# A two-layer convolution-style network on one core: the attention of two images written as one stage instead of two blocks

## The chip, the cores and the metric

One Trainium2 chip, one of its cores. The metric is device time in microseconds (us) of the whole kernel, one launch. Before the change the median of 3 runs is 4517.93 us (4510.86 to 4522.47).

## What is computed

The input x is [2, 256, 64, 64] in fp32: two images of 256 channels and L = 4096 positions. Layer 0 is a selective-scan block, layer 1 is attention with 8 heads of 32 channels, each behind a group norm and with a residual. Cut to what matters here:

```
def _gn(v, G=32, eps=1e-5):                 # per image: mean and variance of each group of 8 channels
    ...
    return ((g - m) / jnp.sqrt(s + eps)).reshape(v.shape)

x = x + _L0_conv_ref(_gn(x), ...)            # layer norm, projection, convolution, scan, gate, MLP
x = x + _L1_conv_ref(_gn(x), qkv_w, qkv_b, 8)

def _L1_conv_ref(x, qkv_w, qkv_b, num_heads):
    qkv = jnp.einsum('bchw,oc->bohw', x, qkv_w) + qkv_b[None, :, None, None]
    ...
    attn_logits = jnp.einsum('bhci,bhcj->bhij', q, k) * scale
    attn_weights = jax.nn.softmax(attn_logits, axis=-1)
    out = jnp.einsum('bhij,bhcj->bhci', attn_weights, v)
```

## The kernel before

**Layer 0** (`mamba_stage`, L257) works through 16 tiles of 512 positions, 8 of each image. All its work is registered as tasks with a cost, a due time and their data dependences (`Plan.add`, L134); `Plan.order` (L180) then simulates the engines and writes out one fixed order for each engine. An engine that stands in front of an instruction whose input is missing also holds everything behind it. Ahead of the plan, `first(0, t, 0)` (L328, L343) loads the 8 tiles of image 0 for the group statistics. The ring `yn` has three buffers (L304). Three small set-up inputs (`w_dt32`, `pick32`, `perm`, L369 to L375) borrow them, and the plan's own load of the first data tile (`front`, L493) takes the first that comes free. The 8 statistics tiles of image 1 (L875) and the late weights (`load_late`, L416) are SyncE tasks of the plan behind that load.

In the last tiles of image 1 the plan also has the group norm and the q, k and v projections of **image 0** for layer 1 (`qkv`, L686), which are written to DRAM scratch.

**Layer 1** is `attention_block` (L931), called twice. For image 0 it has `prepared=True` and loads what layer 0 wrote (`load_prepared`, L1059). For image 1 `prepare` (L985) first makes q, k and v from x: for each of 8 tiles, load x (`load_x`), normalise it with the group-norm scales (L998), project keys and queries (`project`, L1002: 8 matmuls each, q and k split into two halves and written to DRAM) and values (`project_values`, L1026). The tiles it uses are in a pool of its own, opened for the preparation.

Then comes a loop over S = 512 slots of one image. In a slot, TensorE makes the logits of four heads for one block of 128 keys and 512 queries (`logits`, L1098, two PSUM tiles of the ring `s`, which has three buffers) and multiplies the exponentials of the slot before with the values (`values`, L1137). ScalarE makes the exponentials (L1122), VectorE and GpSimd add up the softmax sums (`add_up`, L1151). 32 slots make an output tile. Its end (`finish`, L1178: sums, reciprocal, residual, store) is a generator which the loop advances by one piece in some of the later slots (`Slots`, L60).

The group-norm scales of image 1 (`group_norm_scales`, L30) are such a generator too, started in slot 34 of image 0 (L1217): two small matmuls and Ln and Exp on ScalarE (L56, L57).

All calls stand in `manual_schedule` blocks: within a block the order on each engine is the program's. Instructions of different blocks, and those outside any block, are interleaved by the framework. When a pool is closed, what is allocated there next waits until the old tiles' last users are done.

Of the kernel before, what the change touches and what calls it, by code (L numbers as in the profile page):

```python
# [19 lines left out]
P = 128  # L20
T = 512
# [8 lines left out]
def group_norm_scales(nc, small, psum_tile, stats, gmat, eps_t, out):  # L30

    KC = stats.shape[1]
    mv = [small.tile([P, 2], F32, name=f"gn_mv{k}") for k in range(KC)]
    e = [small.tile([P, 2], F32, name=f"gn_e{k}") for k in range(KC)]
    out += [small.tile([P, 2], F32, name=f"gn_sc{k}") for k in range(KC)]
    for k in range(KC):
        nc.vector.bn_aggr(mv[k], stats[:, k, :, :].rearrange("p a s -> p (a s)"))
    yield 3  # L40
    ps = psum_tile()
    for k in range(KC):
        nc.tensor.matmul(ps[:, 0, k : k + 1], lhsT=gmat, rhs=mv[k][:, 0:1], start=True, stop=True)
    for k in range(KC):
        nc.vector.tensor_copy(out[k][:, 0:1], ps[:, 0, k : k + 1])


    for k in range(KC):
        nc.vector.tensor_sub(e[k][:, 0:1], mv[k][:, 0:1], out[k][:, 0:1])
        nc.vector.scalar_tensor_tensor(e[k][:, 1:2], e[k][:, 0:1], e[k][:, 0:1], mv[k][:, 1:2], ALU.mult, ALU.add)  # L50
    yield 3
    ps = psum_tile()
    for k in range(KC):
        nc.tensor.matmul(ps[:, 0, k : k + 1], lhsT=gmat, rhs=e[k][:, 1:2], start=True, stop=True)
    for k in range(KC):
        nc.scalar.activation(e[k][:, 0:1], ps[:, 0, k : k + 1], AF.Ln, bias=eps_t)  # L56
        nc.scalar.activation(out[k][:, 1:2], e[k][:, 0:1], AF.Exp, scale=-0.5)  # L57
# [199 lines left out]
def mamba_stage(ctx, tc, xs, stats_out, consts, w, outs, scratch):  # L257
# [88 lines left out]


# [134 lines left out]
    def front(i):  # L482
# [4 lines left out]
        yn = d.yn = Buf(r_yn, KC)  # L487
# [5 lines left out]
        add("SP", due - 46, 1.7, lambda: nc.sync.dma_start(yn.tile, image_tile(xs[b], t)), [], [yn], lands=3.3)  # L493
# [437 lines left out]
def attention_block(ctx, tc, b, stats, consts, w, out, scratch, range_t, prepared, ahead):  # L931
# [9 lines left out]
    C, L = out.shape  # L941
# [4 lines left out]
    x = scratch.image(b)  # L946

    p2 = ctx.enter_context(tc.tile_pool(name=f"l1p2{b}", bufs=2))
    wp = ctx.enter_context(tc.tile_pool(name=f"l1w{b}", bufs=1))
    ps_s = ctx.enter_context(tc.tile_pool(name=f"l1pss{b}", bufs=3, space=PSUM))  # L950
    ps_2 = ctx.enter_context(tc.tile_pool(name=f"l1ps2{b}", bufs=1, space=PSUM))
    ps_o = ctx.enter_context(tc.tile_pool(name=f"l1pso{b}", bufs=1, space=PSUM))
# [8 lines left out]
    kp = ctx.enter_context(tc.tile_pool(name=f"l1k{b}", bufs=NT))  # L961
    ep = ctx.enter_context(tc.tile_pool(name=f"l1e{b}", bufs=5))
    ec = ctx.enter_context(tc.tile_pool(name=f"l1c{b}", bufs=2))
    keys = {}
    queries = {}

    def load_keys(g, t, queue=nc.sync):


        k = keys[g, t] = (kq if g and t == 0 else kp).tile([P, 4, T], F32R, name="k")  # L970
        load_stack(queue, k, scratch.qk[b * KG + g, 1, t], 1)

    def load_queries(i, queue=nc.sync):
        if i < KG * NT:
            g, t = divmod(i, NT)
            q = queries[i] = p2.tile([P, 4, T], F32R, name="q")
            load_stack(queue, q, scratch.qk[b * KG + g, 0, t], 0)
# [3 lines left out]


    FIRST = 3

    def prepare():  # L985

        w_qkv, gn = ahead
        with tc.tile_pool(name=f"l1p{b}", bufs=2) as pp:
            xn = {}

            def load_x(t):
                if t < NT:
                    xn[t] = pp.tile([P, KC, T], F32, name="xn")
                    nc.sync.dma_start(xn[t], x.rearrange("(k p) l -> p k l", p=P)[:, :, bass.ts(t, T)])

            def normalise(t):
                for c in range(KC):
                    nc.vector.tensor_scalar(  # L998
                        xn[t][:, c, :], xn[t][:, c, :], gn[c][:, 0:1], gn[c][:, 1:2], ALU.subtract, ALU.mult
                    )  # L1000

            def project(t, i):  # L1002


                pm = s_tile()
                for m in range(KC):
                    for c in range(KC):
                        nc.tensor.matmul(  # L1008
                            pm[:, m, :],
                            lhsT=w_qkv[:, c, bass.ds(i * C + m * P, P)],  # L1010
                            rhs=xn[t][:, c, :],
                            start=(c == 0),
                            stop=(c == KC - 1),
                        )
                halves = pp.tile([P, 2, KC, T], F32R, name="halves")
                for m in range(KC):
                    bias = b_qkv[:, i * KC + m : i * KC + m + 1]
                    nc.scalar.activation(halves[:, 0, m, :], pm[:, m, :], AF.Identity, bias=bias)
                    nc.vector.scalar_tensor_tensor(
                        halves[:, 1, m, :], pm[:, m, :], bias, halves[:, 0, m, :].bitcast(F32), ALU.add, ALU.subtract  # L1020
                    )
                    nc.sync.dma_start(
                        scratch.qk[b * KG + m, i, t].rearrange("s c h t -> (c h) s t"), halves[:, :, m, :].bitcast(F32)
                    )

            def project_values(t):  # L1026
                pm = s_tile()
                flat = pm.rearrange("p a t -> p (a t)")
                for j in range(T // P):
                    for c in range(KC):  # L1030
                        nc.tensor.matmul(
                            flat[:, bass.ts(j, C)],
                            lhsT=xn[t][:, c, bass.ts(j, P)],
                            rhs=w_qkv[:, c, 2 * C : 3 * C],
                            start=(c == 0),
                            stop=(c == KC - 1),
                        )
                nc.scalar.copy(v[:, bass.ts(t, T // P), :].rearrange("p s c -> p (s c)"), flat)

            with tc.manual_schedule():  # L1040
                load_x(0)
                load_x(1)
                normalise(0)
                for t in range(NT):
                    project(t, 1)
                    if t + 1 < NT:
                        normalise(t + 1)
                    project(t, 0)
                    project_values(t)
                    load_x(t + 2)  # L1050

                    if t == 1:
                        load_queries(0)
                    if 0 < t <= FIRST:
                        load_keys(0, t - 1)
                for t in range(FIRST, NT):
                    load_keys(0, t)

    def load_prepared():  # L1059
        def load_values(g, t, queue=nc.sync):  # L1060
            cs = bass.ts(t, T // P)
            queue.dma_start(v[:, cs, g * P : (g + 1) * P], scratch.v[b * KG + g, :, cs, :])

        with tc.manual_schedule():
# [11 lines left out]
    load_prepared() if prepared else prepare()  # L1076

    p1 = ctx.enter_context(tc.tile_pool(name=f"l1p1{b}", bufs=1))
    p3 = ctx.enter_context(tc.tile_pool(name=f"l1p3{b}", bufs=2))
    kq = ctx.enter_context(tc.tile_pool(name=f"l1kq{b}", bufs=1))  # L1080
# [8 lines left out]
    class Slot:  # L1089
        pass  # L1090

    S = KG * NT * NC
    SHARED = [c for c in range(8, NC) if c % 8 in (0, 2, 4, 5, 6)]
    todo = {}
    tiles = {}
    side = Slots()

    def logits(s, half):  # L1098
        if s >= S:
            return  # L1100
        i, c = divmod(s, NC)
        kt, kj = divmod(c * P, T)
        if half == 0:
            todo[s] = Slot()
            todo[s].s, todo[s].e = [], []
        ps = s_tile()
        for j in range(2):
            h = 2 * half + j
            nc.tensor.matmul(  # L1109
                ps[:, j, :], lhsT=keys[i // NT, kt][:, h, kj : kj + P], rhs=queries[i][:, h, :], start=True, stop=True  # L1110
            )
        todo[s].s.append(ps)

    def exponentials(s, half):
        if half == 0 and s % NC < NC - 1:
            k = place(s % NC)
            first = s % NC == 0 or k == 1 and s % NC > 1
            todo[s].chunk = (todo.pop("chunk", None) or chunk()) if first else todo[s - 1].chunk
            e = todo[s].chunk[:, k // 2, :, :, k % 2]
        else:  # L1120
            e = ep.tile([P, 2, T], F32, name="e")
# [303 lines left out]
```

## Time and profile before

| | |
|---|---|
| median of the runs | 4517.93 us |
| the profiled execution: its own time, its span | 4522.6 us, 4520.6 us |
| mean granted TensorE clock | 0.977 |
| busy share of the span: PE, DVE, ACT, POOL | 94%, 87%, 83%, 84% |
| layer 0, until the first logits | 0 to 2123.5 us |
| loop of image 0, until its last values matmul ends | 2123.5 to 3261.8 us |
| first to last matmul of the preparation of image 1 | 3280.7 to 3372.4 us |
| loop of image 1, first exponential to last values matmul | 3373.5 to 4502.2 us |
| end of the span | 4520.6 us |

PE is TensorE (PEld its weight loads), DVE is VectorE, ACT ScalarE, POOL GpSimd, SP SyncE, whose queue issues most transfers. In the time line each row is a start, a duration, an engine, a line of the kernel, an operation with its output and inputs, and in square brackets how long the engine had been idle and what ended that. In the chain each row is a start, a duration and what the end of the kernel was waiting for in that time. In the table by windows each engine has its busy time in the window; then come the granted clock, the busy share of the DMA engines and GB/s.

### The profile page before, as it was taken

To read this page: it belongs to the slowest core of one execution; us is meant where nothing else is said; L and a number is where in the kernel's file an instruction comes from. 1 tells how busy PE (TensorE), PEld (TensorE's weight loads), DVE (VectorE), ACT (ScalarE), POOL (GpSimd) and SP (SyncE) were. 2 spreads that over 40 slices of the span, in tenths; PEclk is the share of its full clock that TensorE was granted. 3 is DMA by queue.
4 is the path that set the end of the run, shared out by engine and by line. 5 is a ranking of instruction groups with operands and counts; after the bars stand their busy time and mean duration, and the time that the engine had idled before them with its cause. 6 is when DMAs were issued, how large, how long until landed. Compare 5 with 4: busy or idle time off the path is not lost.

```text
span 4520.6 us, 53932 instructions
## 1 busy us (share of the span) xinstructions
PE 4252.8 (94%) x18530; PEld 1637.9 (36%) x18530; DVE 3922.2 (87%) x3306; ACT 3766.1 (83%) x4842; POOL 3817.0 (84%) x2251
## 2 busy tenths in 40 slices
PE   5789999999999999988999999999899999999998
PEld 2233333333333333333333333333353333333333
DVE  4999999999999989894889889898838898898988
ACT  4788888888788888873999999999749999999997
POOL 2999999999999999994788888888718888888887
PEclk8899999999999999999999999999999999999999
DMA  5233333333443434446110040100081110401100
GB/s 192 94 115 104 111 124 121 127 126 127 143 155 132 139 122 143 140 151 168 32 27 23 22 102 17 26 24 22 10 262 50 45 28 18 101 17 26 29 20 8
DMA packets 173065, 389.24 MB, mean 86 GB/s; under 512 B 24176, under 2 KB 50544, under 8 KB 164592
## 3 DMA queue, kind: packets, MB, share of 16 engines
q1 hardware_dynamic: 171904, 383.37, 27.5%
q10 hardware_dynamic: 880, 2.36, 0.2%
q8 instruction: 147, 2.41, 0.2%
q14 instruction: 134, 1.10, 0.1%
HBM read 292.34 MB, written 93.32 MB: 85 GB/s over the span
## 4 chain that ended last, share of the span: by engine, by line
PE 64%; POOL 12%; DVE 9%; issue 6%; ACT 5%; DMA 3%; SPq 0%; POOLq 0%; DVEq 0%; ACTq 0%
PE s L1109 26%; PE po L1143 24%; PE mm L437 8%; POOL h L837 6%; DVE h L831 5%; POOL dbu L826 3%; PE y L863 2%; ACT L242 2%; ACT da L820 1%; DVE bn L826 1%; PE mm L669 1%; PE mm L633 1%; PE s L1008 1%; PE bn L437 1%; DMA dtu_rep<-dtu_dram 1%
## 5 line engine op out<-in xcount | busy, mean ns | idle before, releaser
L1135 DVE TENSOR_REDUCE chunk<-chunk 128x1024 f32<-128x4096 f32 x288 | 1269.8, 4409 | 217.0 <-ACT chunk L1122 217.0
L1176 POOL TENSOR_TENSOR acc_p<-acc_p,e 128x1024 f32<-128x1024 f32 x480 | 1150.9, 2398 | 148.5 <-ACT e L1122 129.2
L1122 ACT ACTIVATE chunk<-s 128x1024 f32<-128x1024 f32 x992 | 1117.1, 1126 | 181.6 <-PE s L1109 140.3
L837 POOL TENSOR_TENSOR h<-h,c 128x1024 f32<-128x1024 f32 x512 | 1206.0, 2365 | 40.3 <-ACT state L834 28.3
L1109 PE MATMUL s<-q,k 128*128 128x512 f32 x4096 | 1230.2, 422 | 6.7 <-ACT chunk L1122 3.1
L1143 PE MATMUL po<-chunk,v 128*32 128x512 f32 x3968 | 1112.9, 636 | 0.0
L1143 PE MATMUL po<-e,v 128*32 128x512 f32 x4224 | 1080.3, 605 | 0.0
L1122 ACT ACTIVATE e<-s 128x1024 f32<-128x1024 f32 x1056 | 1073.9, 1020 | 7.3 <-PE s L1109 6.6
L1109 PEld LDWEIGHTS s<-q,k 128*128 128x128 f32 x4096 | 689.5, 188 | 1009.9 <-issue 905.7
L820 ACT ACTIVATE da<-dt_rep,neg_a 128x512 f32<-128x512 f32 x1024 | 690.7, 701 | 131.9 <-DVE h L831 108.2
L1174 POOL TENSOR_TENSOR acc_p<-acc_p,e 128x512 f32<-128x512 f32 x480 | 629.4, 1311 | 162.7 <-ACT e L1122 140.0
L831 DVE TENSOR_TENSOR_SCAN h<-da,state,dbu 128x512 f32<-128x512 f32 x512 | 650.2, 1273 | 44.6 <-POOL dbu L826 41.5
L831 DVE TENSOR_TENSOR_SCAN h<-da,state,bn 128x512 f32<-128x512 f32 x512 | 646.7, 1263 | 11.6
L826 POOL TENSOR_TENSOR dbu<-dtu_rep,b 128x512 f32<-128x512 f32 x384 | 485.8, 1275 | 22.2 <-DMA dtu_rep<-dtu_dram 17.9
L242 ACT ACT_TABLE_LOAD x332 | 426.0, 1283 | 6.5 <-PEq L1415 0.7
L437 PE MATMUL bn<-proj,pick 112*128 112x512 f32 x512 | 294.4, 591 | 116.0 <-DVE h L831 115.4
L863 PE MATMUL y<-h,sum 128*32 128x512 f32 x2048 | 361.0, 633 | 40.0 <-POOL h L837 39.8
L826 DVE TENSOR_TENSOR bn<-dtu_rep,bn 128x512 f32<-128x512 f32 x512 | 348.2, 680 | 41.4 <-PE bn L437 24.0
L1173 DVE TENSOR_TENSOR acc<-acc,e 128x512 f32<-128x512 f32 x448 | 309.5, 691 | 24.2 <-ACT e L1122 13.9
L1143 PEld LDWEIGHTS po<-chunk,v 128*32 128x32 f32 x3968 | 142.9, 108 | 362.6 <-issue 351.3
L437 PE MATMUL mm<-yn,w_in 128*128 128x512 f32 x512 | 252.4, 619 | 10.3 <-ACT yn L526 9.1
L437 PE MATMUL mm<-yn,w 128*128 128x512 f32 x512 | 245.4, 609 | 8.0 <-ACT hid L658 5.7
(136 smaller groups left out, 4055.8 us busy)
## 6 DMA issues: line engine op xcount, KB each, us to landing
dt_rep<-dt_dram SPq DMA_DIRECT2D x128, 512.0 KB, 5.1
dtu_rep<-dtu_dram SPq DMA_DIRECT2D x128, 512.0 KB, 5.5
q<-qk_dram SPq DMA_DIRECT2D x124, 256.0 KB, 4.8
k<-qk_dram SPq DMA_DIRECT2D x62, 512.0 KB, 8.4
b<-bc_dram SPq DMA_DIRECT2D x64, 256.0 KB, 3.1
c<-bc_dram SPq DMA_DIRECT2D x64, 256.0 KB, 3.7
dt_dram<-dt SPq DMA_DIRECT2D x64, 256.0 KB, 2.0
dtu_dram<-lw SPq DMA_DIRECT2D x64, 256.0 KB, 2.5
```

Of the source, the lines that this page charges most:

```text
L242: self.nc.scalar.preload_act_table_set(self.TABLES[task.table])
L437: nc.tensor.matmul(out, lhsT=lhsT, rhs=rhs, start=(i == 0), stop=(i == len(pairs) - 1))
L820: nc.scalar.activation(da[j].tile, dt.tile[:, j, :], AF.Exp, scale=scale)
L826: engine.tensor_mul(out.tile, dtu.tile[:, j, :], rows.tile)
L831: nc.vector.tensor_tensor_scan(h.tile[:, j, :], da[j].tile, dbu.tile, initial, ALU.mult, ALU.add)
L837: nc.gpsimd.tensor_tensor(h.tile, h.tile, rows_c.tile.unsqueeze(1).to_broadcast([P, 2, T]), ALU.mult)
L1109: nc.tensor.matmul(ps[:, j, :], lhsT=keys[i // NT, kt][:, h, kj : kj + P], rhs=queries[i][:, h, :], start=True, stop=True)
L1122: nc.scalar.activation(e, todo[s].s[half], AF.Exp, scale=SCALE)
L1135: nc.vector.tensor_reduce(out, terms, AX.XY, ALU.add)
L1143: nc.tensor.matmul(tiles[i].po[h * D : (h + 1) * D, :], lhsT=v[:, c, g * P + h * D : g * P + (h + 1) * D], rhs=todo[s].e[h // 2][:, h % 2, :],
L1174: nc.gpsimd.tensor_add(acc_p[:, 1, :], acc_p[:, 1, :], eb[:, 1, :])
L1176: nc.gpsimd.tensor_add(acc_p, acc_p, eb)
```

## The change

The two calls become one function, `attention`, with one set of pools for both images and one `manual_schedule` block for the whole of layer 1. The preparation of image 1 no longer has a pool: its x tiles lie in a query buffer and in `e` buffers, its q and k halves in `chunk` buffers of the loop. Its first loads, first normalisation and first projection stand in the last slots of image 0's loop (`run`), and the first logits and exponentials of image 1 ahead of its last value projection. `finish` of image 0's last tile is advanced by the preparation (`side.run()`). The group-norm scales start in slot 1 of image 0 and use the PSUM buffer `a2`; a table set is preloaded on ScalarE at the head of the stage. At the end of `finish` the two range maxima come after the store, and the last product of the kernel is on VectorE. In layer 0 the load of the first data tile moves out of the plan, to just behind the 8 statistics loads of image 0.

```
@@ group_norm_scales
-    yield 3
+    yield 2
     ps = psum_tile()
...
-        nc.vector.scalar_tensor_tensor(e[k][:, 1:2], e[k][:, 0:1], e[k][:, 0:1], mv[k][:, 1:2], ALU.mult, ALU.add)
-    yield 3
+        nc.vector.tensor_mul(e[k][:, 1:2], e[k][:, 0:1], e[k][:, 0:1])
+        nc.vector.tensor_add(e[k][:, 1:2], e[k][:, 1:2], mv[k][:, 1:2])
+    yield 2
     ps = psum_tile()
...
+    yield
     for k in range(KC):
...
@@ mamba_stage
         for t in range(NT):
             first(0, t, 0)
 
+        first_yn = Buf(r_yn, KC)
+        first_yn.tile, first_yn.given = r_yn.make(), True
+        r_yn.given.append(first_yn)
+        nc.sync.dma_start(first_yn.tile, image_tile(xs[0], 0))
...
-        yn = d.yn = Buf(r_yn, KC)
+        yn = d.yn = Buf(r_yn, KC) if i else first_yn
...
-        add("SP", due - 46, 1.7, lambda: nc.sync.dma_start(yn.tile, image_tile(xs[b], t)), [], [yn], lands=3.3)
+        if i:
+            add("SP", due - 46, 1.7, lambda: nc.sync.dma_start(yn.tile, image_tile(xs[b], t)), [], [yn], lands=3.3)
@@ attention_block -> attention
+    def load_x(t):
+        if t >= NT:
+            return
+        if t < 2:
+
+            if t == 0:
+                xn["q"] = p2.tile([P, 4, T], F32R, name="q").bitcast(F32)
+            xn[t] = xn["q"][:, KC * t : KC * t + KC, :]
+        else:
+            xn[t] = ep.tile([P, KC, T], F32, name="e")
+        nc.sync.dma_start(xn[t], scratch.image(1).rearrange("(k p) l -> p k l", p=P)[:, :, bass.ts(t, T)])
...
+        halves = chunk().rearrange("p q h t k -> p q (h t k)").rearrange("p q (m t) -> p q m t", t=T)
...
+    def prepare(image):
+
+        for t in range(NT):
+            if t > 0:
+                project(t, 1)
+                side.run()
+            if t + 1 < NT:
+                normalise(t + 1)
+            project(t, 0)
+            side.run()
+            if t == NT - 1:
+                for half in range(2):
+                    image.logits(0, half)
+                    image.exponentials(0, half)
+            project_values(t)
+            side.run()
+            load_x(t + 2)
+
+            if t == 1:
+                image.load_queries(0)
+            if 0 < t <= FIRST:
+                image.load_keys(0, t - 1)
+        for t in range(FIRST, NT):
+            image.load_keys(0, t)
...
@@ finish
-        at = b * KG * NT + i
-        nc.vector.tensor_reduce(range_t[:, 0, at : at + 1], sums, AX.X, ALU.max)
-        yield 2
...
-        nc.vector.tensor_reduce(range_t[:, 1, at : at + 1], r, AX.X, ALU.max)
-        nc.gpsimd.tensor_mul(po, po, r)
+            (nc.vector if b == 1 and i == KG * NT - 1 else nc.gpsimd).tensor_mul(po, po, r)
...
+            nc.sync.dma_start(out[g * P : (g + 1) * P, cols], res)
+            at = b * KG * NT + i
+            nc.vector.tensor_reduce(range_t[:, 0, at : at + 1], sums, AX.X, ALU.max)
+            nc.vector.tensor_reduce(range_t[:, 1, at : at + 1], r, AX.X, ALU.max)
@@ the loop
+        def run():
+            s = 0
+            while s <= S or b == 1 and side.waiting:
+                i, c = divmod(s, NC)
+                if s < S:
...
+                    if s > 0 or b == 0:
+                        exponentials(s, 0)
+                        exponentials(s, 1)
...
+                if b == 0 and s == S - 8:
+                    load_x(0)
+                    load_x(1)
+                if b == 0 and s == S - 4:
+                    normalise(0)
+                if b == 0 and s == S:
+                    project(0, 1)
+                if 0 < s <= S:
+                    values(s - 1)
+                    if c == 0:
+                        side.start(side.now, finish(i - 1))
+                side.run()
+                logits(s + 1, 0)
+                logits(s + 1, 1)
+                if s < S:
+                    add_up(s)
+                s += 1
...
     with tc.manual_schedule():
...
+        nc.scalar.preload_act_table_set(Plan.TABLES["exp"])
+        images = [image(b) for b in range(2)]
+        images[0].load()
+        nc.sync.dma_start(w_qkv, w["qkv_wT"].rearrange("(k p) f -> p k f", p=P))
+
+        side.start(1, group_norm_scales(nc, wp, lambda: ps_2.tile([P, T], F32, name="gn_ps", tag="a2"), stats[1], gmat, eps_t, gn))
+        for half in range(2):
+            images[0].logits(0, half)
+        images[0].run()
+        prepare(images[1])
+        images[1].run()
```

## The prediction

> **What bounds the kernel now.** I read the shares of busy time and the 40 slices first (PE 94%; a dip in slice 29, at about 3260 to 3390 us), then the table by windows over that dip, then the chain through it, then time lines of two other places that the diff touches: slots 34 to 44 of image 0, where the group-norm scales are, and the first 50 us.
>
> The turn from image 0 to image 1, by windows of 25 us:
> ```profile
> 3250.00:3275.00 25.00, 13.72 (x74) 4.06 (x72) 19.75 (x17) 9.97 (x10) 11.45 (x9) 0.79 0.01 3
> 3275.00:3300.00 25.00, 19.33 (x48) 10.02 (x49) 6.59 (x11) 5.14 (x7) 0.00 (x0) 0.80 0.49 168
> 3300.00:3325.00 25.00, 24.29 (x81) 15.01 (x79) 7.65 (x12) 8.21 (x11) 0.00 (x0) 1.00 1.00 293
> 3325.00:3350.00 25.00, 21.10 (x57) 11.43 (x58) 8.56 (x14) 7.30 (x10) 0.00 (x0) 0.93 1.00 309
> 3350.00:3375.00 25.00, 24.57 (x81) 14.72 (x79) 8.66 (x14) 10.77 (x14) 0.00 (x0) 1.00 0.80 282
> 3375.00:3400.00 25.00, 25.00 (x141) 9.42 (x140) 14.56 (x5) 23.45 (x25) 21.85 (x11) 1.00 0.97 216
> ```
> TensorE stands idle first at a clock of 0.79 with the DMA engines empty (share 0.01); then both are nearly full. The chain says what it waits for:
> ```profile
> 3260.82 2.36 POOL acc_p L1176
> 3263.18 8.69 issue
> 3271.90 1.27 POOL po_sb L1207
> 3273.20 0.76 DVE res L1210
> 3273.98 2.09 DMA out<-res
> 3276.21 3.58 DMA xn<-x_dram
> ...
> 3314.07 12.10 DMA xn<-x_dram
> ...
> 3329.86 9.00 DMA xn<-x_dram
> ```
> The whole end of the last output tile, down to its store, is awaited before x of image 1 is even loaded: its pool is the old one's memory. Later, two loads of x stand 12.1 and 9.0 us behind stores and key loads.
>
> Everywhere else in the two loops TensorE sets the pace: in the chain a slot is 1.05 us of values and 1.13 us of logits, 2.18 in all. 511 slots and 15 times 1.07 us of sums (L1194) make 1130 us; image 1 took 1128.7 from first exponential to last values matmul, image 0 1136.2. The 7.5 us more are the group-norm scales:
> ```profile
> 2215.53 1.28 ACT L56 ACT_TABLE_LOAD   x1
> 2217.11 1.28 ACT L57 ACT_TABLE_LOAD   x1
> 2218.62 1.28 ACT L56 ACT_TABLE_LOAD   x1
> 2220.20 1.28 ACT L57 ACT_TABLE_LOAD   x1
> 2220.23 1.22 PE L1109 MATMUL s<-q,k 128*128 128x512 f32 x2 [2.63 <-ACT gn_e L56]
> ```
> Ln and Exp alternate between table sets, 6.16 us of ScalarE in all, while TensorE starves.
>
> And the start:
> ```profile
> 24.60 0.37 SPq L493 DMA_DIRECT2D yn<-in_x  x1
> 28.34 0.81 ACT L491 ACTIVATE yn<-yn,scales 128x512 f32<-128x512 f32 x1 [6.19 <-issue]
> 44.27 2.06 DVE L331 BATCH_NORM_STATS2 stats_in<-h 128x6 f32<-128x512 f32 x3 [6.62 <-DMA h<-in_x]
> 46.25 1.39 DVE L522 SCALAR_TENSOR_TENSOR yn<-yn,gamma,mm 128x512 f32<-128x512 f32 x2
> ```
> SP idles from 19.97 to 24.60 (the last use of `w_dt32`, L401, ends at 24.57) before the first data tile is loaded, and all image-1 statistics loads stand behind it. L522, which starts the first projections, stands in VectorE's order behind statistics whose tile lands at 44.2.
>
> **The turn, part by part.** I count on TensorE, from the end of image 0's last values (3261.8) to the first values of image 1 (3375.2): 113.4 us. The work in it: a projection of 8 matmuls takes 3.44 us (L1008 x16 in 6.88), a value projection 3.45, so 10.32 per tile and 82.6 for eight; one sums group 1.07; two slots of logits 2.26. Together 85.9, so 27.5 us are lost.
>
> Taken away: the wait for the old pools (3263.2 to 3280.7, less the sums group) with the half-clock start behind it (first two projections 9.20 instead of 6.88), and the start of the loop behind `project_values` (ScalarE's copy 1.01, exponential 0.99). That is about 3.3 + 1.1 + 13.5 + 2.3 + 0.7 = 20.9. The cover for `finish` is the preparation: its vector pieces (three additions and copies 2.6, sums 0.7, reciprocals 3.4, residual 0.75, maxima 1.4) and the GpSimd product lie in an engine busy 8 of 25 us; without that cover they are 10 us again. x(0) and x(1) load in slot 504, at a DMA share of 0.04, and their normalisation (1.0 us of VectorE) falls where VectorE has 0.6 us free per three slots: nothing on TensorE, as values don't wait for it.
>
> Kept: the DMA stall. Per tile there are 2.1 MB of stores, 0.5 of x, and in tiles 1 to 3 1 MB of keys (2 with queries). 10.3 us at the 309 GB/s of the full window carry 3.2 MB. That backlog delays x(4) and x(5) by 2.7 and 2.4 us, with 1.8 of half clock behind. The new x buffers lift only the wait for the projection of t before load(t+2); SP issues that load at 3314.07 right behind the last store (3313.98) anyway, so I leave 6.9, less 1 because the sums group now gives tile 1 a microsecond: 6.
>
> Added: `project_values(7)` takes the third `s` buffer while the halves of `project(7,0)` are still read. In tile 1 these ended 3.2 us after their projection; 1.13 of logits fill a part: 2.1 us of wait on TensorE, with logits(1) and values(0) queued behind. Lost after: 6 + 2.1 = 8.1; saved 27.5 - 8.1 = 19.4. Check by bytes: 31.7 MB move between 3275 and 3400, of which 5 (keys 3 to 7) may come later; 26.7 MB at 309 GB/s are 86 us, from the first store at about 3266 to 3352, just below TensorE's own 3355.8. So the DMA engines forbid much more.
>
> [...] Here the 2.1 us gap before 3339.5 was already followed by a slow group (8.83 for 6.88). [...]
>
> **The scales.** They move from slots 34 to 40 to slots 1 to 6: same four products (about 0.5 us of TensorE twice). The two VectorE products of 2.4 us (L50) become two short operations each (the neighbouring L49 takes 0.17); VectorE did not hold TensorE there, so 0. The price is the tables. If the preload stands where it is written, Ln and Exp need no switch (4 x 1.28 and what follows, 6.5 us), and the first exponential's load (1.28 at 2124.29) leaves the path: 7.4 saved. But the preload has no operand to wait for, and the framework issues such things early: the memset of L424, written behind all weights, runs at 0.99; a query load of layer 1 (L927, 2083.40) stands on ACT's queue ahead of layer 0's L722 (2087.10). So I expect it at the head of the program, where it covers nothing: 0, with the ends 0 and 7.4 (a gain only; a stray load costs 1.28 of an idle ScalarE). [...]
>
> **The start.** The load of the first tile moves ahead of 16 small and large loads on SP, each 0.5 later in issue and up to 1.7 in arrival (0.5 MB at 309 GB/s); they are awaited at 22 us at the earliest. What is late next: the scales' last step and the mean stand behind image-1 statistics in VectorE's order, and L522 behind x tile 6. So the gain is how much earlier those loads begin. SP's gap of 4.6 us goes, and 0.5 MB leaves that queue: up to 5. But `perm` now asks for the fourth `yn` buffer of three and gets one only after L401, at 24.6; if it stands ahead of the statistics loads, the gap stays and only the 1.6 of the moved bytes is gained. VectorE's `diag_d` (0.9) and all behind it wait for `perm`; that has 5.9 us of cover (rstd ends at 40.4, L522 starts at 46.25). Ends 0 and 5; I take 4, since the DMA share between 20 and 24 us is 0.18.
>
> **The end.** In the chain 0.69 (L1200) and about 0.65 (VectorE 0.69 for GpSimd 1.27) leave, two maxima of 0.69 come ahead of `range_top`: 0.
>
> **Sum.** 4522.6 - 19.4 - 0 - 4 = 4499.2 for the profiled execution, which lies 4.7 above the median; on the median 4494.5.
>
> **Rivals.** About 0.3% (13.6 us) is what a measurement of this kernel can tell from no change.
> - *Likeliest (50%)*: as above, 4494.5; own range 4489 to 4501.
> - *The preload holds* (17%): for it, that it is written at the head of the block; against it, L424 and L927. 7.4 more: 4487.
> - *The DMA stall goes too* (14%): if the smoother start spreads the traffic; against it, share 1.00 for 50 us. 6 to 8 more: 4487; with the preload 4479.
> - *The DMA engines set the turn and `perm` blocks SP* (11%): 26.7 MB at the 282 of the last window are 95 us, 14 saved there, 0 at the start: 4504, within or just outside 0.3%.
> - *Slower* (4%): the plan of layer 0 is simulated anew without its first SP task. Its 16 tiles of about 129 us run on four nearly full engines, and L831 waited for GpSimd's `dbu` up to 3.6 us at a time. If the new order puts one such wait into every tile, 16 x 3.6 = 57.6 us are lost against 23.4 won: 4552. It decides from 1.5 us per tile. Against it: in the plan's arithmetic the scales, not the tile, are ready last, so times meet again after the first centring.
> - The rest (4%) is scatter between these.
>
> So 4494.5, range 4478 to 4508; faster 0.88, same 0.08, slower 0.04.
>
> **What would show it.** Right: no gap over 4 us on TensorE between the images, the first values of image 1 some 91 us behind the last of image 0 (94 less the one projection that now precedes these); x(4) and x(5) still landing 9 us late; four table loads at L56 and L57, now about 15 us into the loop, and one at the first exponential; L522 at about 42. Wrong: no table loads there; DMA waits gone, or x in the slots of image 0 holding its logits; tiles of layer 0 of another length.

## The result and the profile after

The median fell from 4515.1 us (six runs, 4510.9 to 4522.5) to 4501.0 (six runs, 4498.3 to 4507.3): ratio 0.9968, 95% interval 0.9955 to 0.9981. That is 14.1 us, where 23.4 were predicted; 4501.0 lies inside the range of 4478 to 4508, 6.5 us above the forecast of 4494.5. The profiled execution of after took 4507.3 us, its span is 4505.2 (before 4522.6 and 4520.6), both at a mean granted clock of 0.977.

I divided both spans into five stages at instructions of TensorE. "Image 0's loop" ends with the values of its last slot but one, so that the projection that the change puts ahead of the last values falls into the turn in both kernels. The second column of before is a second profiled execution (run `e1_before_again`); the column "after's kin" is the spread over those experiments that left the stage alone.

| stage, us | before | before again | after | after's kin | predicted change | measured |
|---|---|---|---|---|---|---|
| layer 0, to the first logits | 2123.5 | 2118.4 | 2115.5 | 2109.5 to 2118.6 | -4 | -6.6 (mean of 2 to mean of 10) |
| loop of image 0 | 1136.7 | 1136.6 | 1141.5 | 1141.5 to 1142.5 | 0 | +4.8 |
| turn, to the first values of image 1 | 115.0 | 113.8 | 96.8 | 92.9 to 97.9 | -19.4 | -18.2 |
| loop of image 1 | 1127.0 | 1127.0 | 1129.7 | 1129.7 to 1129.9 | 0 | +2.7 |
| behind the last values | 18.4 | 19.2 | 21.7 | 21.3 to 21.8 | 0 | +2.9 |

So the part that was meant to gain gained as forecast, and 10.4 us came in at three places that the forecast had at nothing. First the turn, the table by windows of after (PE, PEld, DVE, ACT, POOL busy, granted clock, DMA share, GB/s):
```profile
3250.00:3275.00 25.00, 25.00 (x101) 11.28 (x98) 17.10 (x18) 12.07 (x15) 7.49 (x5) 1.00 0.35 123
3275.00:3300.00 25.00, 25.00 (x82) 15.26 (x81) 9.99 (x16) 7.52 (x10) 0.00 (x0) 1.00 0.94 286
3300.00:3325.00 25.00, 22.44 (x64) 12.30 (x63) 10.37 (x16) 7.99 (x11) 1.26 (x1) 0.93 1.02 307
3325.00:3350.00 25.00, 22.02 (x65) 12.56 (x64) 10.70 (x17) 10.08 (x13) 0.00 (x0) 0.96 0.73 272
```
The hole is gone: TensorE is busy for all of the first 50 us, where before it had 13.7 and 19.3 of 25. What is left stands in the second 50 us, at a DMA share of 1.02 and then 0.73. TensorE's time line of after there:
```profile
3303.38 8.83 PE L1016 MATMUL s<-e,w_qkv 128*128 128x512 f32 x16 [2.56 <-DVE e L1006]
...
3326.96 7.13 PE L1016 MATMUL s<-e,w_qkv 128*128 128x512 f32 x16 [0.79 <-DVE e L1006]
...
3347.54 5.41 PE L1037 MATMUL s<-w_qkv,e 128*128 128x256 f32 x16 [2.19 <-DVE chunk L1027]
```
The first and the last are the waits that the prediction kept and added: x(4), which took 12.1 us from its issue at 3290.61 to landing (2.56), and `project_values(7)`, which waits for an `s` buffer (2.19). Both groups run at half clock behind their wait (granted 0.50 from 3303.82 to 3307.23 and from 3348.19 to 3351.60): 8.83 for 7.13, and 5.41 for 3.72 in other runs. The middle wait (0.79) is no DMA wait: x(6), issued at 3318.61, had landed after 6.7 us, but VectorE worked until 3326.4 on the last pieces of `finish` (`L1225`, `L1228`, `L1229`), which stand ahead of the normalisation.

The scales, in the time line of after, 19 us behind the first logits:
```profile
2134.65 1.28 ACT L58 ACT_TABLE_LOAD   x1
2136.22 1.28 ACT L59 ACT_TABLE_LOAD   x1
2137.74 1.28 ACT L58 ACT_TABLE_LOAD   x1
2139.32 1.28 ACT L59 ACT_TABLE_LOAD   x1
2141.82 0.73 PE L1131 MATMUL s<-q,k 128*128 128x512 f32 x2 [3.38 <-ACT chunk L1144]
```
All four loads are there, and one of 1.28 at the first exponential (2116.31): the preload covers none of them.

The start, VectorE and SyncE in the time line of after:
```profile
24.13 0.35 SPq L382 DMA_DIRECT2D yn<-in_perm x1
...
42.27 2.63 DVE L333 BATCH_NORM_STATS2 stats_in<-h 128x6 f32<-128x512 f32 x4 [6.52 <-DMA h<-in_x]
44.82 1.39 DVE L530 SCALAR_TENSOR_TENSOR yn<-yn,gamma,mm 128x512 f32<-128x512 f32 x2
```
L530 is L522 of before: 44.82 instead of 46.25. `perm` holds SyncE until 24.13, and VectorE still waits 6.5 us for an x tile (6.62 before), only 2.0 us earlier.

And a new row near the end, on VectorE in after:
```profile
4480.93 0.06 DVE L1294 MEMSET all_rows<- 128x1 f32 x1 [3.06 <-PE s L1131]
4480.98 0.70 DVE L1191 TENSOR_TENSOR acc<-acc,e 128x512 f32<-128x512 f32 x1
4481.59 4.41 DVE L1153 TENSOR_REDUCE acc_sb<-chunk 128x1024 f32<-128x4096 f32 x1
```
A memset of 128 numbers, for the range test behind everything, stands in VectorE's order ahead of the last sums and waits 3.06 us for the last logits.

### The profile page after: what moved, and what is told of

It reads as the page before. It is cut to its first block, busy times and chain, and to the rows that moved or that the text cites. A ratio compares the mean times of both kernels' runs of the same rounds, so it can differ in the third digit from the quotient of the medians.

```text
span 4505.2 us, 53942 instructions
## 1 busy us (share of the span) xinstructions
PE 4257.1 (94%) x18530; PEld 1642.2 (36%) x18530; DVE 3890.9 (86%) x3309; ACT 3768.4 (84%) x4842; POOL 3807.4 (85%) x2249
## 3 DMA queue, kind: packets, MB, share of 16 engines
q10 hardware_dynamic: 880, 2.36, 0.2%
## 4 chain that ended last, share of the span: by engine, by line
PE 57%; DVE 4%; ACT 3%; POOL 3%; issue 2%; DMA 1%; DVEq 0%; POOLq 0%; SPq 0%; ACTq 0%
PE s L1131 25%; PE po L1161 24%; PE mm L444 3%; DVE h L839 2%; POOL h L845 2%; ACT da L828 1%; ACT L244 1%; PE mm L677 1%; PE s L1016 1%; PE y L871 1%; POOL dbu L834 1%; PE sums_ps L1212 1%; DVE bn L834 1%; PE mm L641 0%; PE bn L444 0%
## 5 line engine op out<-in xcount | busy, mean ns | idle before, releaser
L1144 ACT ACTIVATE chunk<-s 128x1024 f32<-128x1024 f32 x992 | 1121.5, 1131 | 185.5 <-PE s L1131 139.9
L1192 POOL TENSOR_TENSOR acc_p<-acc_p,e 128x512 f32<-128x512 f32 x480 | 620.2, 1292 | 129.3 <-ACT e L1144 106.6
L444 PE MATMUL bn<-proj,pick 112*128 112x512 f32 x512 | 296.4, 595 | 112.2 <-DVE h L839 111.6
L444 PE MATMUL mm<-yn,w_in 128*128 128x512 f32 x512 | 254.7, 625 | 10.3 <-ACT yn L534 9.1
```

The lines of the kernel that those rows point to most:

```text
L444: nc.tensor.matmul(out, lhsT=lhsT, rhs=rhs, start=(i == 0), stop=(i == len(pairs) - 1))
L1144: nc.scalar.activation(e, todo[s].s[half], AF.Exp, scale=SCALE)
L1192: nc.gpsimd.tensor_add(acc_p[:, 1, :], acc_p[:, 1, :], eb[:, 1, :])
```

## The experiments

Twelve kernels. Eleven ran once, with a profile; the stages repeat so closely (the table) that changes of more than 1 us can be read from one trace, except in layer 0, whose 16 tiles alone differ by 5 us between two executions of one program, and in the turn (see below). My theory after the comparison: the turn as predicted; the rest is the new addresses of tiles, a memset in the wrong memory, and tables that the preload doesn't hold.

**Before again**, no edit.

> The kernel before, unchanged, profiled a second time. It separates what the change did from what differs between two executions. In the first profiles a slot of the steady loop took 2.180 us before and 2.187 after, in every tile of both images (about 5.7 us in all), and the last tile of layer 0 ran 4.4 us shorter after. If the slot time belongs to the execution or to the chip it ran on, this run shows something other than 2.180, or the other runs of this call show 2.180; if it belongs to the program, this run shows 2.180 again. Layer 0 to the first logits: 2123.5 us again if the program fixes it; nearer to 2119 if the 4.4 us of its last tile was chance.

Measured: 4516.9 us. A slot took 2.180 us again in every tile of both images but the one with the scales, and the last tile of layer 0 (last output product to first logits) 40.4 us after 40.8. Both belong to the program. The rest of layer 0 took 4.7 us less than in the first execution: that part does not.

**The addresses.**
```
+    ahead = ctx.enter_context(tc.tile_pool(name="next", bufs=1))
+    w_qkv = ahead.tile([P, KC, 3 * C], F32, name="w_qkv")
     p2 = ctx.enter_context(tc.tile_pool(name="l1p2", bufs=2))
...
-    w_qkv = wp.tile([P, KC, 3 * C], F32, name="w_qkv")
...
-        side.start(1, group_norm_scales(nc, wp, ...
+        side.start(1, group_norm_scales(nc, ahead, ...
```

> After, with the weights of the projections and the small tiles of the scales in a pool of their own that is opened first, as before: the tiles v, q and everything above them then lie at the addresses of the kernel before, and the lowest address belongs to the weights and no longer to q. No instruction of the loops changes. Theory (the changed addresses cost time in two places): a slot takes 2.180 us again instead of 2.187 (2.8 us less in each image's loop), and the memset of all_rows, which now lies in the weights, no longer waits for the last logits, so that the time behind the last values is 18.4 us instead of 21.7 (3.2 less); span 9 us under after. Rival for the slots: not the addresses but the execution, or the order of VectorE's reductions, then a slot stays at 2.187 and only the tail changes. Rival for the tail: the last tile's product on VectorE sets it, then 21.7 stays.

Measured: 4490.3 us. The groups of after, and then of this run (busy us, mean ns, idle before):
```profile
L1144 ACT ACTIVATE chunk<-s 128x1024 f32<-128x1024 f32 x992 | 1121.5, 1131 | 185.5 <-PE s L1131 139.9
...
L1161 PE MATMUL po<-chunk,v 128*32 128x512 f32 x3968 | 1121.7, 642 | 0.0
```
```profile
L1145 ACT ACTIVATE chunk<-s 128x1024 f32<-128x1024 f32 x992 | 1116.1, 1125 | 183.2 <-PE s L1132 142.8
...
L1162 PE MATMUL po<-chunk,v 128*32 128x512 f32 x3968 | 1112.6, 636 | 0.0
```
The same instructions on the same data are 6 ns shorter each, and a slot is 2.180 us instead of 2.187. Image 1's loop took 1126.8 (-2.9), image 0's 1137.1 (-4.3; besides the slots, some 1.4 around the scales), the end 18.5 (-3.2). On VectorE the last `TENSOR_REDUCE` now starts 4.1 us ahead of the last values' end, as in before, and not 2.0. The theory holds in both places: some 10 us of the loss are only where tiles lie. With the old addresses the new place of the scales costs 0.5 us.

**Which address.** v at its old place, q not: the scales' tiles and the weights are allocated just below v.
```
+    small = {f"gn_{n}{k}": wp.tile([P, 2], F32, name=f"gn_{n}{k}") for n in ("mv", "e", "sc") for k in range(KC)}
...
+    w_qkv = wp.tile([P, KC, 3 * C], F32, name="w_qkv")
     v = wp.tile([P, NC, C], F32, name="v")
```

> After, with v at the address of the kernel before (the weights and the scales' small tiles now lie below it), while q and everything else stay where after has them. With all the old addresses a slot took 2.180 us again and the time behind the last values was 18.5. Theory (it is v's address that costs the 7 ns of a slot): 2.180, while the tail stays at 21.6, since all_rows still lies in q. Rival (it is q's address): 2.187. If neither moves, it was the address of all_rows, which no slot touches, or something that I don't see.

Measured: 4497.2 us; slots of 2.182 and 2.191 us in turn, 2.1865 on average; image 1's loop 1129.6, behind the last values 21.3. v's address does something (the slots now alternate, and the exponentials took 1128 ns, the matmuls 645), but it gives back 0.1 us of the 2.9. So q's address, or the two together, is the cause. q alone was not tried, and how an address makes a matmul and an exponential slower no run shows.

**The tables.**
```
-        nc.scalar.preload_act_table_set(Plan.TABLES["exp"])
         images = [image(b) for b in range(2)]
         images[0].load()
+        nc.scalar.preload_act_table_set(Plan.TABLES["exp"])
```

> After, with the preload of the activation tables issued behind the loads of image 0 that stand on ScalarE's queue instead of ahead of everything in the stage. In after four loads of 1.28 us stood between the Ln and Exp of the scales and one ahead of the first exponential. Theory (as the first statement of the stage the preload runs long before, and layer 0's activations undo it): now it holds, none of the five loads is there, ScalarE's part of the scales is 5.1 us shorter, TensorE no longer idles 3.4 us at their end, and image 0's loop takes 3 to 7 us less than after's 1146.1. Rival (the set that was loaded doesn't serve both functions, or the loads are placed by the function alone): all four remain and the loop is within 1 us.

Measured: 4497.4 us. Image 0's loop took 1134.0 instead of 1141.5. (The 1146.1 of the expectation counts to the end of the last values, in this measure 1138.6 here: 7.5 less either way.) ScalarE's time line of this run:
```profile
2133.64 0.28 ACT L58 ACTIVATE gn_e<-gn_ps,eps_t 128x1 f32<-128x1 f32 x1
2133.94 0.20 ACT L59 ACTIVATE gn_sc<-gn_e 128x1 f32<-128x1 f32 x1
...
```
No load stands between these two, nor in the second pair (2134.05 and 2134.33), nor at the first exponential; the one load of the stage ran at 2101.5, in ScalarE's idle time, at the preload's own line. In after none of the 337 table loads stands at the preload's line, and before has 337 as well. So behind transfers on ScalarE's own queue the preload kept its place, and as the first statement of its block it left no load at all; what became of it there no trace shows.

**The scales late again**, with the new form, and **the old form** at the early place:
```
-        side.start(1, group_norm_scales(..., lambda: ps_2.tile([P, T], F32, name="gn_ps", tag="a2"), ...
+        side.start(NC + 2, group_norm_scales(..., lambda: s_tile()[:, 0, :], ...
```

> After, with the scales of the second image computed at slot 34 again and in a tile of the s ring, as before; their new short operations are kept. Theory (the early place, not the new form, costs the difference): the first five slots take 10.9 us again instead of 19.8, and some 7.5 us are lost at slots 34 to 40, so image 0's loop is about 2 us shorter than after's 1141.4. Rival (the form: four short VectorE operations that took 2.3 us beside GpSimd instead of two): the loss goes along to the new place and is 9 to 10 us there, image 0's loop is within 0.7 us of after's.

```
-        nc.vector.tensor_mul(e[k][:, 1:2], e[k][:, 0:1], e[k][:, 0:1])
-        nc.vector.tensor_add(e[k][:, 1:2], e[k][:, 1:2], mv[k][:, 1:2])
+        nc.vector.scalar_tensor_tensor(e[k][:, 1:2], e[k][:, 0:1], e[k][:, 0:1], mv[k][:, 1:2], ALU.mult, ALU.add)
```

> After, with the square and the sum of the scales in one scalar_tensor_tensor per channel block again, as before, at the early slot. In after the two-operand ops of that chain that met a GpSimd instruction took 2.25 to 2.33 us, one GpSimd instruction (2.40) each, and the second pair of products waited 1.42 us for the last of them. Theory (the chain is as long as the GpSimd instructions it has to let pass; one op fewer per block is one wait fewer): the products no longer wait, and image 0's loop is 1.4 to 3 us shorter than after's 1146.1. Rival (only the four table loads count): within 0.7 us.

Measured: 4510.0 and 4506.0 us. Late, slots 1 to 7 took 15.0 us instead of 23.1, but slots 34 to 42 took 30.8 instead of 20.5; image 0's loop is 1142.4. The loss goes along, and the theory that the early place costs time is wrong. With the old form the early slots took 22.9 instead of 23.1, and the loop 1142.3: the theory of fewer waits for GpSimd is wrong too. Both loops are some 1 us longer than that of after (the rivals had 0.7 at most), but within its kin. Why the late place lost 10.3 us here and only 7.3 in before stays open.

**`perm` in memory of its own.**
```
-    perm = r_yn.make()[:, 0, 0:P]
+    perm = wp.tile([P, P], F32, name="perm")
```

> After, with the tile perm in memory of its own instead of in the yn ring. In after SyncE stood at the load of perm until 24.13 us, and the five loads of the first images' x behind it went out at 24.5 to 26.5. Theory (that wait keeps back what the early yn load gave): SyncE no longer waits, the loads go out about 2.5 to 3 us earlier, and the first projection starts at about 43 to 44 us instead of 46.4. Rival: VectorE's own work bounds the start, whose centring op waited for a DMA only until 42.27; then the projection moves by under 1 us. Layer 0's later tiles move along by the same amount; nothing else changes.

Measured: 4505.3 us. SyncE loads `perm` at 18.2 and goes on with the x tiles at 21.75, yet the first projection starts at 45.80 instead of 46.37. VectorE, in this run:
```profile
41.71 2.64 DVE L333 BATCH_NORM_STATS2 stats_in<-h 128x6 f32<-128x512 f32 x4 [6.58 <-DMA h<-in_x]
```
The theory's 43 to 44 is wrong; the 0.6 us, under 1 us as the rival had it, are within the scatter of the runs with an unchanged start (45.4 to 47.0). The rival's reason, VectorE's own work, doesn't fit the wait above. The last three x tiles go out from 31.0 on, behind the three late weights and a wait of 2.3 us for VectorE, and are awaited as long as in after. That these two set the start is read from the time lines; no run removed them.

**The weights' load first.**
```
+        nc.sync.dma_start(w_qkv, w["qkv_wT"].rearrange("(k p) f -> p k f", p=P))
         images[0].load()
-        nc.sync.dma_start(w_qkv, w["qkv_wT"].rearrange("(k p) f -> p k f", p=P))
```

> After, with the load of the projections' weights (786 KB) issued ahead of the first queries, keys and values instead of behind them. From the last output product of layer 0 to the first logits it took 40.8 and 40.4 us in two executions of the kernel before and 36.4 to 36.6 us in four kernels of after's kind. Theory (the weights' load, which in the kernel before stood ahead on the queue, shared the DMA engines with the last tile's stores and the first loads): this stretch takes about 40.5 us again. Rival (another cause, such as the order of the loads of queries and keys on ScalarE's queue): it stays at 36.5. Everything else as after.

Measured: 4505.2 us; the last tile of layer 0 took 39.2 us. That is 2.6 to 2.8 of the 4 us that after gained there. The theory gives the greater part; the rest I did not find.

**The early pieces of the preparation undone.**
```
-                if b == 0 and s == S - 8:
-                    load_x(0)
-                    load_x(1)
-                if b == 0 and s == S - 4:
-                    normalise(0)
-                if b == 0 and s == S:
-                    project(0, 1)
...
+        load_x(0)
+        load_x(1)
+        normalise(0)
```

> After, but the first two x tiles are loaded, the first normalised and the first projection made only when image 0's loop has ended, as in the kernel before; the shared tiles and the first logits ahead of the last value projection stay. After's turn took 92.2 us (89.4 to 92.8 in its kin), before's 113.4 and 112.2. Theory (most of the gain is in the three pieces that move up beside the last slots: the load of x 3.6, the normalise 1.0 and their pipeline's fill, and no wait for memory of the ended loop remains): the turn takes 7 to 10 us more than after's, 99 to 102 us. Rival (the early pieces are the whole gain): the turn is 112 us again. Second rival (the shared tiles alone are the gain, and DMA sets the rest): under 95 us.

Measured: 4514.1 us; from last to first values 98.1 us, where after's kin need 88.3 to 93.2 and before 113.4 and 112.2. In the stages of the table the turn is 99.7: some 14 to 15 us come from the shared tiles and what goes with them, 5 to 7 from the early pieces (against the four kin of 88.3 to 89.8, which ran at full clock in the stall as this run did). TensorE idled 3.8 us ahead of its first projection, where it had idled 13.65. Neither rival holds, and the theory only in part: its 99 to 102 us are nearly met, but the early pieces are the smaller part of the gain and not most of it.

**Keys 1 and 2 behind the last projection.**
```
-    FIRST = 3
+    FIRST = 1
```

> After, with the loads of image 1's second and third keys issued behind the last projection instead of between the projections. In after TensorE idled 2.56 us and ran 2.0 us longer at half clock in the middle of the turn, behind x loads that stood in the DMA queues behind keys. Theory (the key loads cause that stall): it goes, the turn is 4 to 6 us shorter (86 to 88 us), but if the keys come late, slot 4 or 8 of image 1 waits for them and gives some of it back. Rival (the x loads wait for their e tiles or for their issue, not behind the keys): the turn stays within 89 to 93 us.

Measured: 4501.3 us; 85.6 us from last to first values. TensorE's time line:
```profile
3302.16 7.13 PE L1016 MATMUL s<-e,w_qkv 128*128 128x512 f32 x16 [0.52 <-DVE e L1006]
...
3343.38 3.72 PE L1037 MATMUL s<-w_qkv,e 128*128 128x256 f32 x16 [2.19 <-DVE chunk L1027]
```
Of the DMA stall 0.5 us is left, and image 1's loop is as long as after's: the keys were early by more than they need. Against the four kin at full clock that is 2.7 to 4.3 us, against after 6.7. The value projection waits 2.19 us as in after, but runs at full clock.

**The first logits behind the last value projection.**
```
-            if t == NT - 1:
-                for half in range(2):
-                    image.logits(0, half)
-                    image.exponentials(0, half)
             project_values(t)
             side.run()
+            if t == NT - 1:
+                for half in range(2):
+                    image.logits(0, half)
+                    image.exponentials(0, half)
```

> After, with the first logits and exponentials of image 1 behind the last value projection instead of ahead of it. In after the last value projection waits 2.2 us for an s buffer that the first exponentials free, and runs at half clock behind that wait (2.0 us more). Theory (that wait is the price of the early logits, and their gain is that the exponentials run beside the value projection): the turn stays within 1.5 us of after's 89.4 to 92.8, as the first values now wait for the exponentials, some 2.2 us, instead. Rival (the early logits are worth the 2.2 us of two exponentials and more): 93 to 96 us. Second rival (the wait costs more than they bring): 86 to 88 us.

Measured: 4501.0 us; 87.35 us from last to first values, no wait for an `s` buffer. That is within the second rival's numbers: the early logits cost more than they bring. From the start of the last projection to the first values it took 13.2 us, as in before, and 14.7 in each of the four kin at full clock: 1.5 us, and 1.7 more where the wait brings half clock.

**Four edits together**: the addresses, the preload, the keys, the logits.

> After with four edits together: the addresses of the kernel before, the preload behind image 0's first loads, the second and third keys behind the last projection, the first logits behind the last value projection. Theory (the four act in different stages and add up): image 0's loop 1146.1 - 2.9 - 7.5 = 1135.7, the turn 85.55 less 1 to 3 = 82.5 to 84.5, image 1's loop 1126.9, the tail 18.5, layer 0 within 2109 to 2119 as in all runs so far; a span near 4478, ratio to the kernel before 0.992. Rival (late keys and late logits are the same slack told twice: with the keys behind the last projection, the logits that follow the value projection wait for key 0 or the query, or slots 4 and 8 wait for keys 1 and 2): the turn is 86 or more, or slots 4 and 8 of image 1 are longer than 2.2 us, and the ratio is 0.993 to 0.994.

Measured, in five rounds: 4481.9 us (4480.2 to 4487.8) against 4516.5 before, ratio 0.9926, interval 0.9912 to 0.9939. Image 0's loop 1132.0 (in the measure of the expectation 1136.6), 84.3 us from last to first values, image 1's loop 1127.0, the end 19.35, layer 0 2112.8. Every stage but image 0's loop and the end, 0.9 each above it, is where the theory had it. The two edits of the turn brought 6.7 and 4.9 us alone and 7.9 together. That is no shared slack: after, from which all three are counted, ran twice at half clock (1.7 us each) and none of these runs did; counted once, 6.7 + 4.9 - 3.4 make 8.2. This is the best version of the study: the change as written gets 14 us, with these four edits 35.

## Why the prediction was right, and where it was not

- **The turn**: -19.4 predicted, -18.2 measured, 92.2 us from last to first values against 91. The steps hold one by one: no gap above 4 us, the wait for the old pools gone, the DMA stall and the half clock behind it kept (2.56 + 1.70, with the 0.79 about 5 where 6 were left), 2.2 for the `s` buffer where 2.1 were estimated. Two terms are missing, both small: the half clock behind that last wait, 1.7 us, and the 0.79, for which `finish` was not wholly covered. That the early logits cost 1.5 us more than they bring shows only in the run with late logits.
- **"The DMA engines forbid much more" and "the DMA stall goes too" (14%)**: no run shows the first to be wrong. Its 86 us count from the first store and contain keys 0 to 2. With all of these loads in place the run with late logits took 86.8 us from its first store (3260.86) to the first values, and the second execution of before 85.9 (from 3282.81). With keys 1 and 2 later the same sum is 24.7 MB or 80 us (an estimate at the same 309 GB/s), and that run took 85.0. The second did not come true in after, but moving 2 MB behind the last projection was enough for it.
- **The scales**: 0 predicted, +0.5 measured at equal addresses. The outcome was right: at the head of its block the preload covered nothing, and four loads remained. That it ran at the head of the program is not shown. Its price if it holds is near: 7.4 forecast (its two terms, 6.5 and 1.28, make 7.8), 7.5 measured. The two VectorE products did not become short: in after one of each pair took 2.25 and 2.33 us, which cost nothing, as the old form showed. The four loads don't belong to the two pairs as such: in run `e10_preload`, behind the one load at 2101.51, both pairs (2133.64 and 2134.05) and the first exponential (2116.74) ran without one.
- **The start**: -4 predicted, -1.4 measured in the profiled pair (-1.9 between the means). I chose 4 between 0 and 5 because the DMA share was 0.18 from 20 to 24 us, and named `perm` as what would spoil it. It was there, but it was not the limit: without it the gain grows by no more than 0.6. What failed is "the gain is how much earlier those loads begin". In that run the four loads behind `perm` began 2.2 us earlier; the last three, which VectorE awaits, stand behind the late weights and a wait for VectorE and began only 0.7 us earlier.
- **Not in the sum**: 4 us at the end of layer 0. The weights' load had stood ahead of the last tile's transfers; ScalarE waited 6.44 us for one of them, and 2.85 in after:
```profile
2095.53 0.69 ACT L658 ACTIVATE hid<-mm,b 128x512 f32<-128x512 f32 x1 [6.44 <-DMA qk_dram<-hid]
```
```profile
2087.97 0.69 ACT L666 ACTIVATE hid<-mm,b 128x512 f32<-128x512 f32 x1 [2.85 <-DMA qk_dram<-hid]
```
  The prediction has no term for what a moved load had held up; putting it back brought 2.6 to 2.8 of the 4 us back.
- **The loops and the end at 0**: this is the step that failed, by 10.4 us, of which some 0.5 are the scales. The prediction has no term for the slots: their instructions are indeed unchanged, but not their durations; and a tile that is allocated behind the stage (`all_rows`) fell into q instead of the weights, so that a memset waited for the last reader of q, with the last sums behind it on VectorE. In the prediction the end was summed from the operations of `finish` alone.

The two misses of opposite sign, 4 gained and 10.4 lost, make most of the 9 us between forecast and result. That they partly cancel is luck: without the 4 us, which no term had, the median would have been some 4505, still in the range but near its edge. By its number the rival of 4504 was the nearer one, but not by its mechanism: with the same loads the turn went down to 87.35 us and not to 95. The slower rival (the plan of layer 0 with a wait in every tile) did not occur: from the first projection to the last output product layer 0 took 2035.0 and 2029.8 us before and 2032.8 after.

## What to carry to other kernels

When tiles move to other pools, look for two things that no line of the diff shows: which later allocation now lies in whose memory, and whether a steady loop's instructions still have their durations; compare the mean of each group, not only their count. Look in the trace whether a preload left its load where you wrote it: here it did so behind transfers on its own queue, and not as the first statement of its block. In a stage that is full of DMA traffic, first ask which transfers are due last.

## What the runs showed of the hardware

- The same matmul took 642 or 636 ns, the same exponential 1131 or 1125, and a slot 2.187 or 2.180 us, with nothing changed but where tiles lie (after and run `e2_layout`): 0.3% of a loop. Whether a wait in the memory is behind that, and of which engine, these rows don't show.
- In these runs half clock behind a wait isn't a matter of its length alone. The group behind the x stall ran slow after waits of 2.56 (after), 2.75 (`e4_gn_late`), 3.35 (`e5_w_first`) and 3.58 us (`e12_gn_stt`): 8.69 to 8.83 for 7.13. It ran at full clock after 1.69 (`e3_perm`), 2.54 (`e10_preload`) and 2.65 (`e2_layout`). In the kernel before the longer wait was followed by full clock and the shorter one by half:
```profile
3326.80 7.13 PE L1008 MATMUL s<-xn,w_next 128*128 128x512 f32 x16 [2.51 <-DVE xn L998]
...
3339.49 8.83 PE L1008 MATMUL s<-xn,w_next 128*128 128x512 f32 x16 [2.10 <-DVE xn L998]
```
  In the traces of before and after the granted clock changes 66 and 68 times, and within each trace the changes lie whole multiples of 3.413 us apart, to 0.02 us: in after's turn at 3303.82, 3307.23, 3348.19 and 3351.60. Divided into stretches between such points, after has:
```profile
3300.41:3303.82 3.41, 0.85 (x3) 0.31 (x3) 1.91 (x5) 0.33 (x1) 0.00 (x0) 1.00 0.99 187
3303.82:3307.23 3.41, 3.41 (x5) 1.35 (x4) 2.23 (x3) 1.59 (x2) 0.34 (x1) 0.50 0.96 294
```
  The wait of 2.56 us lies within one stretch, and the next one is granted 0.50. Before's 2.10 us too lie within one (3336.09 to 3339.51; the next is granted 0.50), while a border at 3325.85 divides its 2.51 us into 1.56 and 0.95, and the clock stays at 1.00. In the turns of these two traces the stretches at full clock with 2.10 to 2.63 us of idle TensorE (2.10, 2.19, 2.56, 2.63) were followed by half clock, and none with 1.56 or less. Over the rest of the two traces, behind their first 35 us, the border is less sharp: falls from 1.42 us of idle on, none missing from 2.0 on. So here it mattered where a gap fell and not only how long it was. The four runs that were slow at the stall were also slow in the last value projection behind its wait of 2.19 us (5.33 to 5.41 where the group stands whole in the trace; 3.72 in the others); in after that wait lies within the stretch ahead of 3348.19, 13 such steps (44.37 us) behind the first fall. With these two groups, each 1.6 to 1.7 us longer, the turn of after's kin fell into two sets, 88.3 to 89.8 and 92.2 to 93.2 us from last to first values.
- The six VectorE operations of the scales on 128 x 1 numbers (L49 to L51 of after, 2125.89 to 2131.56) took 0.15 or 0.16 us, three times, and 0.56, 2.25 and 2.33 us; these three ended within 0.02 us of the end of a GpSimd addition (2.36 to 2.40 us each) that was under way. In before the two products of L50, 2.43 and 2.37 us, ended likewise.
